# Reordering the loads at the start of a selective scan, and moving one copy from VectorE to ScalarE

## The chip, the cores and the metric

The kernel runs on one core of a Trainium2 chip. The metric is the device time of one execution in microseconds (us). The engines are TensorE (PE, matmuls), VectorE (DVE), ScalarE (ACT), GpSimd (POOL) and SyncE (SP); SP computes nothing here and issues most of the DMA transfers. Each engine works through its own instructions in order, and engines wait for one another by semaphores.

## The reference, cut to what matters

Two layers of a language model follow each other: a Mamba block with a 4-bit quantised feed-forward network, and an attention block with a mixture-of-experts network. The changed lines all lie in the Mamba block. It has two sequences (b = 0, 1) of 512 tokens with 512 features, 1024 inner channels and 16 states per channel:

```python
x = x + _layernorm(_L0_attn_ref(_layernorm(x), ...))      # the Mamba block, then three more
# inside _L0_attn_ref:
proj = hidden_states @ W_in.T
x, gate = (proj[..., :D_IN], proj[..., D_IN:])             # D_IN = 1024
xc = conv_b + sum(conv_w[:, j] * xpad[:, j:j + L, :] for j in range(4))
x = silu(xc)
ssm = x @ W_x.T
ts, Bm, Cm = rms(ssm[..., :32]), rms(ssm[..., 32:48]), rms(ssm[..., 48:])
dt = softplus(ts @ W_dt.T + b_dt)
def step(state, inp):                                      # over the 512 tokens
    dt_t, B_t, C_t, u_t = inp
    state = state * exp(dt_t[..., None] * A) + (dt_t * u_t)[..., None] * B_t[:, None, :]
    return state, einsum('bdn,bn->bd', state, C_t)
y = (ys + x * D) * silu(gate)
return y @ W_out.T
```

## The kernel before

Everything is in float32. Channels lie on the 128 partitions, so a sequence has 8 chunks of channels (c = 0 to 7), and tokens lie along the free dimension. The 16 states go in 8 groups (gi) of two. A scan step s handles one group of one chunk of one sequence: 2 x 8 x 8 = 128 steps.

*The head* runs before the scan and handles sequence 0: its tokens are loaded (`load_x(0)`, L83), normalised and transposed; for each chunk PE projects (L613), ACT and DVE do the convolution and the SiLU, and PE collects the "ranks" dt, B and C of all chunks in one PSUM bank. Beside it DVE, POOL and ACT dequantise words of the feed-forward weights and store them to DRAM (L233, L288, L299, L304). Gate 0 is projected in full (L639), and the first two of the four matmuls of gate 1 are done while DVE normalises the ranks (`half_gate`, L650). The normalised ranks are transposed on PE (L536). `ranks_out` (L539) then copies the dt rows to `dtT` on ACT (L541) and the B and C rows to `bc` on DVE (L542), and stores `bc` to DRAM as `scr` (L544). From there `states` (L547) loads each group of B or C back, broadcast to all partitions: 512 KB into a tile of 128 x 2 x 512. Sixteen of these transfers (eight B, eight C) are queued on SP one after the other; only group 0's product takes B from a matmul instead (`B0`, L688 to L693). Behind them on SP stand the four tiles of sequence 1's tokens (`load_x(1)`, L667) and then the loads of the last cut of the words. At most eight transfers of SP are in flight: each reuses one of eight semaphores and waits for the transfer eight places before it.

*The scan stage* goes through the 128 steps. For each step ACT takes two exponentials into PSUM (`exps`, L1033), DVE multiplies dt*u with B (`times_B`, L1049, reported at L1055) and runs the recurrence as one scan instruction over 1024 elements (`scan`, L1057, reported at L1059), POOL multiplies by C (`times_C`, L1063, L1065), and PE adds the groups up with identity matmuls (`sums`, L1075, L1087). Six `bx` buffers carry a step from DVE over POOL to PE; two `da` tiles carry the exponentials, so that those of step s + 2 wait for scan s. At each new chunk ACT copies dt to PSUM (`new_du`, L1043, L1047) and DVE multiplies it by u (L1053); `fin` (L1093) multiplies the finished chunk by its gate.

Beside the scan a generator (`stream`, L993) gives PE its other work for both sequences in pieces: the gates (`gate`, L751, matmuls at L741), each followed by three ACT instructions and a POOL product (`silu_of`, L712 to L719); the transposes of sequence 1 (L821); its projections; its ranks (`ranks1`, `rows1`, which call `ranks_norm` and `ranks_out` for b = 1); and, once the gates of sequence 0 are used, the output projection with weights `wo` (L897, L953) and the feed-forward network. The norm of sequence 1 (`norm_job`, L793) places one `bn_stats` (L798) on DVE every step from step 5 on. A rough budget (`STEP` = 3.5 us per step and `MM` = 0.86 us per matmul) decides how many pieces of the stream go into each step. In chunk 7 of sequence 0 the broadcasts of sequence 1's B and C follow, each as soon as its tile is free (L1152).

The order of the instructions on PE, ACT, DVE and POOL is exactly the order in which the program traces them (`pin`, L405). SP isn't pinned: `tc.issue_after` sets a lower limit for a transfer, and its place on the queue is found by the scheduler.

Of the kernel before, what the change touches and what calls it, by code (L numbers as in the profile page):

```python
# [18 lines left out]
P = 128  # L19
# [37 lines left out]
def tile_sandwich(  # L57
# [48 lines left out]
    wgt = const.tile([P, KH, NE], F32, name="wgt")  # L106


    def w4(src, name, chunks=KH, cols=PW):
        t_ = wst.tile([P, KH, PW], F32, tag="w4", name=name)  # L110
        nc.sync.dma_start(out=t_[:, :chunks, :cols], in_=src)
        return t_

    def moments(srcs, name):
# [311 lines left out]
    with ExitStack() as mamba:  # L426
# [21 lines left out]
        def mbank(name):  # L448
            return ps_m.tile([P, S], F32, tag="m", name=name)
# [18 lines left out]
        def w_in(part, b, c):  # L468

            key = "w", part, b, c // 2  # L470
            if key not in st:
                st[key] = w4(W_in[part * NCH // 2 + c // 2], f"w_{'xg'[part]}{b}_{c // 2}")
            return st[key]
# [28 lines left out]
        def ranks_norm(b, ps):  # L502

            sq = jrow(f"sq{b}")[:, : TB * N_ROW].rearrange("p (i r n) -> p i r n", i=TB, n=N_ST)
            nc.scalar.activation(sq.rearrange("p i r n -> p i (r n)"), ps, AF.Square)
            yield 2
            ss = stat.tile([P, TB, 3], F32, tag="ss", name=f"ss{b}")
            nc.vector.tensor_reduce(
                ss[:, :, 0], sq[:, :, : R_DT // N_ST].rearrange("p i r n -> p i (r n)"), AX.X, ALU.add
            )  # L510
            nc.vector.tensor_reduce(ss[:, :, 1:], sq[:, :, R_DT // N_ST :], AX.X, ALU.add)
            r = stat.tile([P, TB, 3], F32, tag="rr", name=f"rr{b}")
            nc.vector.tensor_scalar(r[:, :, 0], ss[:, :, 0], 1.0 / R_DT, 1e-6, ALU.mult, ALU.add)
            nc.vector.tensor_scalar(r[:, :, 1:], ss[:, :, 1:], 1.0 / N_ST, 1e-6, ALU.mult, ALU.add)
            yield 1
            if b:
                nc.gpsimd.tensor_tensor(r, r, mhalf3, ALU.pow)
            else:
                nc.scalar.activation(r, r, AF.Sqrt)
                nc.vector.reciprocal(r, r)  # L520
            yield 3
            nb = jrow(f"nb{b}")[:, : TB * N_ROW].rearrange("p (i r) -> p i r", i=TB)
            eng = nc.gpsimd if b else nc.vector
            eng.tensor_mul(
                nb[:, :, :R_DT], ps[:, :, :R_DT], r[:, :, 0:1].to_broadcast([P, TB, R_DT])
            )
            eng.tensor_mul(
                nb[:, :, R_DT:].rearrange("p i (r n) -> p i r n", n=N_ST),
                ps[:, :, R_DT:].rearrange("p i (r n) -> p i r n", n=N_ST),
                r[:, :, 1:3].unsqueeze(3).to_broadcast([P, TB, 2, N_ST]),  # L530
            )
            st["nb", b] = nb
# [6 lines left out]
        def ranks_out(b, pt):  # L539
            bc = st["bc"] = jrow(f"bc{b}")  # L540
            nc.scalar.copy(dtT[b][:R_DT, :], pt[:R_DT])  # L541
            nc.vector.tensor_copy(bc[R_B:N_ROW], pt[R_B:N_ROW])  # L542
            sc = dram.tile([N_ROW - R_B, S], F32, tag=f"scr{b}", name=f"scr{b}")
            nc.sync.dma_start(out=sc, in_=bc[R_B:N_ROW])  # L544
            scr.append(sc)
# [27 lines left out]
        with ExitStack() as p1:  # L573
            dq = pool(p1, "dq", 1)
            dz = pool(p1, "dz", 1)
            ps_1 = pool(p1, "p1mm", 2, PSUM)
            ps_r = pool(p1, "p1r", 1, PSUM)

            def bank1(i, name):
                return mbank(name) if i % 2 else ps_1.tile([P, S], F32, tag="mm", name=name)  # L580

            xT.append(xT_tile("xT0"))
            mvs, rn, xns, tps = {}, {}, {}, {}
            for i in range(TB + 2):
                if i < TB:
                    nm_ = f"m0_{i}"
                    mvs[i] = moments([x[i]], nm_)
                    rn[i] = rstd(mvs[i], nm_, 1)
                if 0 <= i - 1 < TB:
                    j = i - 1  # L590
                    rs = rn[j]
                    nm = minus_mean(mvs[j], rs, f"m0_{j}", 1)
                    xn = jrow(f"xn0_{j}")
                    apply(xn, x[j], rs, nm, 0)
                    tp = tps[j] = bank1(j, f"tp0_{j}").rearrange("p (k t) -> p k t", k=KH)
                    for kc in range(KH):
                        nc.tensor.transpose(tp[:, kc, :], xn[:, ts(kc, P)], ident)
                if 0 <= i - 2 < TB:
                    nc.scalar.copy(xT[0][:, :, ts(i - 2, P)], tps[i - 2])
            nc.scalar.activation(A, ch[:, :, KCONV + 2 :], AF.Exp)  # L600
            zds = zeros(dz, [gate_z, up_z], KH, INTER, "gu")

            apart = [f"gu{CUTS[1][0] * PW}_{j}" for j in range(PACK - 4, PACK)]
            gw.start(dq, zds, lambda n: new_g0(f"w_{n}") if n in apart else None)
            nc.vector.tensor_scalar(A, A, -1.0, None, ALU.mult)
            diag(0)

            pr = ps_r.tile([P, TB, S], F32, tag="psm", name="psm0")[:, :, :N_ROW]
            for c in range(NCH):
                w = w_in(0, 0, c)  # L610
                ps = bank1(c, f"px0_{c}")
                for k in range(KH):
                    nc.tensor.matmul(  # L613
                        ps, w[:, k, ts(c % 2, P)], xT[0][:, k, :], start=(k == 0), stop=(k == KH - 1)
                    )
                    if k == 1 and c >= 2:
                        for i in range(TB):
                            ranks_of(0, c - 2, i, pr)
                uc = u[0][c] = new_u(f"u0_{c}")
                evict_x(c, ps, uc)  # L620
                early = [gw.steps() for _ in range(4 if c == 0 else 0)]
                for word in early:
                    next(word)
                for word in early[:2]:
                    next(word)
                conv(c, ps, uc)
                nc.scalar.activation(uc, uc, AF.Silu)
                for word in early:
                    for _ in word:
                        pass  # L630
                if c:
                    gw.word()
                for _ in range((0, 0, 2, 0, 1, 0, 1, 0)[c]):
                    gw.word(nc.gpsimd)
            for i in range(TB):
                ranks_of(0, NCH - 2, i, pr)
            pg = mbank("pg0_0")
            for k in range(KH):
                nc.tensor.matmul(  # L639
                    pg, w_in(1, 0, 0)[:, k, 0:P], xT[0][:, k, :], start=(k == 0), stop=(k == KH - 1)  # L640
                )
            for i in range(TB):
                ranks_of(0, NCH - 1, i, pr)
            g[0][0] = new_g0("g0_0")
            nc.scalar.activation(g[0][0], pg, AF.Silu)

            root = stat.tile([P, 1], F32, tag="root", name="root", bufs=1)
            nc.scalar.activation(root, half[:, 0:1], AF.Sqrt)

            half_gate = mbank("pg0_1")  # L650
            for k in range(KH // 2):
                nc.tensor.matmul(
                    half_gate, w_in(1, 0, 0)[:, k, P : 2 * P], xT[0][:, k, :], start=(k == 0), stop=False
                )
            for _ in ranks_norm(0, pr):
                pass
            ranks_out(0, ranks_rows(0, bank1(0, "pt0")))

            for gi in range(NGI):
                if gi + 1 < NGI:  # L660
                    states(0, gi + 1, "B")
                states(0, gi, "C")
            last = states(0, 0, "B")
            gw.word()
            dt_out(0, 0, dt_in(0, 0, bank1(0, "pv0_0")))
            with tc.issue_after(last.ins):
                load_x(1)  # L667
            pin()

        g1p = pool(mamba, "mg1", 1)  # L670
# [4 lines left out]
        with ExitStack() as p2:  # L675
# [75 lines left out]
            def gate(b, c):  # L751
                w = w_in(1, b, c)
                if c + 2 - c % 2 < NCH:
                    w_in(1, b, c + 2 - c % 2)
                if (b, c) == (0, 1):
                    turns.append([f"pg{b}_{c}", None])
                    ps = half_gate
                    yield from in_proj(b, ps, w, c % 2, KH // 2)
                else:
                    ps = yield from bank(f"pg{b}_{c}")  # L760
                    yield from in_proj(b, ps, w, c % 2)
                spawn(gate_job(b, c, ps), 2)
# [717 lines left out]
```

## Time and profile before

| What | us |
|---|---|
| Median of 3 runs (957.22 to 958.73) | 957.5 |
| The profiled execution | 955.66 |
| Its span, first to last instruction | 953.7 |
| The head, up to the store of `bc` | 0 to 63.3 |
| Steps 0 to 7, with the first broadcasts | 68.0 to 104.5 |
| Transposes of sequence 1's ranks, DVE's copy of its B and C | 285.7 to 287.6 |
| Last step of sequence 0 on DVE | 326.4 to 328.6 |

The profile is of one execution. Its mean granted TensorE clock is 0.965 of full speed. Times within it are us from the start of the span. A row of a timeline reads: start, length, engine, line, operation, output <- input, count, and in brackets the idle time before it with what ended it. A name such as `bx` stands for all buffers of that name; `xN` counts instructions that were merged. A matmul of the program shows as two records. "SPq" is SP's issuing of a transfer, not the transfer. Tensor names carry no buffer numbers, so the n-th row of a group is told by its place in the order.

### The profile page before, as it was taken

To read this page: it belongs to the slowest core of one execution; us is meant where nothing else is said; L and a number is where in the kernel's file an instruction comes from. 1 tells how busy PE (TensorE), PEld (TensorE's weight loads), DVE (VectorE), ACT (ScalarE), POOL (GpSimd) and SP (SyncE) were. 2 spreads that over 40 slices of the span, in tenths; PEclk is the share of its full clock that TensorE was granted. 3 is DMA by queue.
4 is the path that set the end of the run, shared out by engine and by line. 5 is a ranking of instruction groups with operands and counts; after the bars stand their busy time and mean duration, and the time that the engine had idled before them with its cause. 6 is when DMAs were issued, how large, how long until landed. Compare 5 with 4: busy or idle time off the path is not lost.

```text
span 953.7 us, 7163 instructions
## 1 busy us (share of the span) xinstructions
PE 860.8 (90%) x2188; PEld 385.4 (40%) x2188; DVE 672.4 (71%) x780; ACT 424.1 (44%) x638; POOL 486.8 (51%) x356
## 2 busy tenths in 40 slices
PE   6989778789999889589999999999999998999994
PEld 3433333334533434134434444444544444455441
DVE  5877999999999998999999995535600024525225
ACT  4356675656666655476655640125320013412122
POOL 7746796677877787876877884440000000011002
PEclk9989999888999999889999999999999999999998
DMA  6449111010002854200111103445222231100101
GB/s 201 156 141 376 52 37 38 30 37 30 22 23 91 293 194 142 89 0 0 45 44 45 30 9 125 153 156 198 57 65 74 60 101 44 67 12 23 56 0 44
DMA packets 43816, 80.08 MB, mean 84 GB/s; under 512 B 7774, under 2 KB 20937, under 8 KB 43778
## 3 DMA queue, kind: packets, MB, share of 16 engines
q1 hardware_dynamic: 41506, 73.64, 23.4%
q0 software_dynamic: 1984, 5.47, 1.6%
q10 hardware_dynamic: 288, 0.52, 0.1%
q8 instruction: 17, 0.28, 0.1%
q14 instruction: 21, 0.17, 0.1%
HBM read 68.37 MB, written 11.24 MB: 83 GB/s over the span
## 4 chain that ended last, share of the span: by engine, by line
PE 48%; DVE 24%; issue 9%; POOL 7%; DMA 3%; ACT 2%; SPq 0%; DVEq 0%; POOLq 0%; ACTq 0%
DVE bx L1059 10%; DVE bx L1055 6%; PE py L1087 6%; PE pd L1408 6%; POOL bx L1065 5%; PE pup L1345 5%; PE fo L1198 4%; PE fg L371 4%; PE fu L371 4%; PE fo L1261 3%; PE fu L984 3%; PE fg L984 3%; PE po L1176 3%; PE po L953 2%; DVE u L483 2%
## 5 line engine op out<-in xcount | busy, mean ns | idle before, releaser
L1065 POOL TENSOR_TENSOR bx<-bx,C 128x1024 f32<-128x1024 f32 x128 | 301.8, 2358 | 117.4 <-DVE bx L1059 94.2
L1059 DVE TENSOR_TENSOR_SCAN bx<-da,bx 128x1024 f32<-128x1024 f32 x128 | 291.4, 2277 | 0.1
L1087 PE MATMUL py<-bx,ident 128*128 128x512 f32 x480 | 234.9, 620 | 41.4 <-POOL bx L1065 36.3
L1039 ACT ACTIVATE da<-dt,A 128x511 f32<-128x511 f32 x256 | 176.6, 691 | 170.1 <-DVE bx L1059 163.4
L1087 PEld LDWEIGHTS py<-bx,ident 128*128 128x128 f32 x480 | 90.8, 197 | 168.1 <-issue 91.7
L1055 DVE TENSOR_TENSOR bx<-du,B 128x1024 f32<-128x1024 f32 x127 | 152.8, 1203 | 5.7 <-DMA B<-scr 2.2
L1274 DVE TENSOR_TENSOR it<-it,fu 128x512 f32<-128x512 f32 (+1 forms) x11 | 7.5, 686 | 75.2 <-PE fu L371 75.2
L385 POOL TENSOR_TENSOR sd<-ve,half 128x4 f16<-128x4 f16 x2 | 2.1, 1042 | 110.7 <-DVE ve L383 110.7
L1345 PE MATMUL pup<-hT_l,wup 128*128 128x512 f32 x128 | 57.8, 606 | 0.0
L741 PE MATMUL pg<-xT,w_g 128*128 128x512 f32 x116 | 56.5, 619 | 0.0
L1408 PE MATMUL pd<-wdn,hid 128*128 128x512 f32 x128 | 55.3, 593 | 0.0
L127 POOL TENSOR_TENSOR rs_lo<-ve_lo,mhalf 128x1 f32<-128x1 f32 x8 | 5.4, 680 | 76.7 <-DVE ve_lo L125 76.7
L371 PE MATMUL fg<-hT_f,wg 128*128 128x512 f32 (+1 forms) x88 | 41.9, 614 | 0.7 <-ACT hT_f L171 0.7
L984 PE MATMUL fg<-hT_f,wg 128*128 128x512 f32 (+1 forms) x88 | 42.1, 597 | 0.0
L984 PE MATMUL fu<-hT_f,wu 128*128 128x512 f32 (+1 forms) x88 | 40.7, 592 | 0.0
L483 DVE SCALAR_TENSOR_TENSOR u<-px,ch,u 128x511 f32<-128x511 f32 (+2 forms) x48 | 35.8, 746 | 6.9 <-ACT u L476 5.8
L1261 PE MATMUL fo<-wd,it 128*128 128x512 f32 (+1 forms) x88 | 40.5, 603 | 0.0
L371 PE MATMUL fu<-hT_f,wu 128*128 128x512 f32 (+1 forms) x88 | 39.8, 593 | 0.0
L1198 PE MATMUL fo<-wd,it 128*128 128x512 f32 (+1 forms) x88 | 38.0, 594 | 1.8 <-DMA wd<-wd_d 1.8
L1408 PEld LDWEIGHTS pd<-wdn,hid 128*128 128x128 f32 x128 | 24.2, 190 | 30.7 <-issue 30.1
L1345 PEld LDWEIGHTS pup<-hT_l,wup 128*128 128x128 f32 x128 | 24.3, 193 | 28.8 <-issue 28.8
L1273 ACT ACTIVATE it<-fg 128x512 f32<-128x512 f32 (+1 forms) x11 | 6.6, 597 | 65.7 <-PE fg L371 65.7
(238 smaller groups left out, 1164.8 us busy)
## 6 DMA issues: line engine op xcount, KB each, us to landing
wo<-in_W_outT SPq DMA_DIRECT2D x20, 512.0 KB
B<-scr SPq DMA_DIRECT2D x16, 512.0 KB
C<-scr SPq DMA_DIRECT2D x16, 512.0 KB
wg<-wgu_d SPq DMA_DIRECT2D x10, 512.0 KB
wu<-wgu_d SPq DMA_DIRECT2D x10, 512.0 KB
w_x<-in_W_in SPq DMA_DIRECT2D x8, 512.0 KB
wgu_d<-w_gu POOLq DMA_DIRECT2D x16, 256.0 KB, 2.4
w_g<-in_W_in SPq DMA_DIRECT2D x8, 512.0 KB
```

The costliest lines, as they stand in the source:

```text
L371: nc.tensor.matmul(ps[:m], w[:, kc, e * P : e * P + m], hT[:, kc, :], start=(kc == 0), stop=(kc == KH - 1),)
L741: nc.tensor.matmul(ps, w[:, k, ts(e, P)], xT[b][:, k, :], start=(k == 0), stop=(k == KH - 1))
L984: nc.tensor.matmul(ps[:m], wt[j][a][:, kc, e * P : e * P + m], hT[:, kc, :], start=(kc == 0), stop=(kc == KH - 1),)
L1039: nc.scalar.activation(das[s % 2][:, i, 1:], st["dt", b, c][:, 1:], AF.Exp, scale=A[:, c, n : n + 1])
L1055: nc.vector.tensor_mul(bx, st["du"].unsqueeze(1).to_broadcast([P, NG, S]), Bbs[b][gi])
L1059: nc.vector.tensor_tensor_scan(flat, das[s % 2].rearrange("p n t -> p (n t)"), flat, 0.0, ALU.mult, ALU.add)
L1065: nc.gpsimd.tensor_mul(bxs[s], bxs[s], Cbs[b][s % NGI])
L1087: nc.tensor.matmul(st["y"], ident, bx[:, i, :], start=False, stop=last)
L1198: nc.tensor.matmul(fo[t], its[i][:m, ts(t, P)], w[:m, e], start=(i == 0), stop=(i == len(IC) - 1),)
L1261: nc.tensor.matmul(fo[t], its[i][:m, ts(t, P)], w[:m], start=(i == 0), stop=(i == len(IC) - 1),)
L1345: nc.tensor.matmul(ps, w[:, kc, ts(e, P)], src[kc], start=(kc == 0), stop=(kc == KH - 1))
L1408: nc.tensor.matmul(pd, hid[kc][:, ts(i, P)], wdn[kc], start=(kc == 0), stop=(kc == INT // P - 1),)
```

## The change

Four edits, all in the Mamba block:

- The tokens of sequence 1 are loaded behind the first gate weights (`issued[-1]` is then the load of `w_g0_0`), ahead of the stores and broadcasts of B and C. On SP's queue they move past two loads of gate weights, the store of `scr`, and sixteen broadcasts. The later loads of words and weights keep their order, but for one weight load (`w_x1_2`), which goes ahead of a store of dequantised words (L304) that was in front of it.
- The broadcasts of sequence 0 go B1, B2, C0, B3, C1, B4, C2, ..., B7, C5, C6, C7, B0 instead of B1, C0, B2, C1, B3, C2, ..., B7, C6, C7, B0.
- For sequence 1, `ranks_out` copies the B and C rows on ScalarE, right behind the copy of the dt rows, instead of on VectorE. On DVE the instruction stood between a product with B (group 5 of chunk 6) and the scan of group 4.
- Gate 1 of sequence 0 has three of its four matmuls in the head and one in the scan stage. On PE the last matmul of gate 2 then moves ahead of the dt matmul of chunk 1 (L562); all that follows has the order of before.

```diff
+    issued = []
+
     def w4(src, name, chunks=KH, cols=PW):
         t_ = wst.tile([P, KH, PW], F32, tag="w4", name=name)
-        nc.sync.dma_start(out=t_[:, :chunks, :cols], in_=src)
+        issued.append(nc.sync.dma_start(out=t_[:, :chunks, :cols], in_=src))
         return t_
...
             nc.scalar.copy(dtT[b][:R_DT, :], pt[:R_DT])
-            nc.vector.tensor_copy(bc[R_B:N_ROW], pt[R_B:N_ROW])
+            if b:
+                nc.scalar.copy(bc[R_B:N_ROW], pt[R_B:N_ROW])
+            else:
+                nc.vector.tensor_copy(bc[R_B:N_ROW], pt[R_B:N_ROW])
...
-            half_gate = mbank("pg0_1")
-            for k in range(KH // 2):
+            first_gate = mbank("pg0_1")
+            for k in range(KH - 1):
                 nc.tensor.matmul(
-                    half_gate, w_in(1, 0, 0)[:, k, P : 2 * P], xT[0][:, k, :], start=(k == 0), stop=False
+                    first_gate, w_in(1, 0, 0)[:, k, P : 2 * P], xT[0][:, k, :], start=(k == 0), stop=False
                 )
+            with tc.issue_after(issued[-1].ins):
+                load_x(1)
...
             for gi in range(NGI):
                 if gi + 1 < NGI:
                     states(0, gi + 1, "B")
-                states(0, gi, "C")
+                if gi:
+                    states(0, gi - 1, "C")
+            states(0, NGI - 1, "C")
             last = states(0, 0, "B")
             gw.word()
             dt_out(0, 0, dt_in(0, 0, bank1(0, "pv0_0")))
-            with tc.issue_after(last.ins):
-                load_x(1)
...
-                    ps = half_gate
-                    yield from in_proj(b, ps, w, c % 2, KH // 2)
+                    ps = first_gate
+                    yield from in_proj(b, ps, w, c % 2, KH - 1)
```

## The prediction

> **What bounds the kernel now.** I read the page first, then the waits of VectorE (DVE), then the timelines of SP, DVE, ScalarE (ACT), GpSimd (POOL) and TensorE (PE) around those waits. The page names PE, but as an average over stages:
>
> ```profile
> PE 860.8 (90%) x2188; PEld 385.4 (40%) x2188; DVE 672.4 (71%) x780; ACT 424.1 (44%) x638; POOL 486.8 (51%) x356
> PE 48%; DVE 24%; issue 9%; POOL 7%; DMA 3%; ACT 2%; SPq 0%; DVEq 0%; POOLq 0%; ACTq 0%
> ```
>
> The stretches (length, then busy us of PE, PEld, DVE, ACT, POOL, then granted clock) tell the stage that the change touches:
>
> ```profile
> 58.00:92.00 34.00, 32.06 (x70) 13.12 (x70) 23.59 (x27) 24.99 (x39) 19.33 (x12) 0.90 0.82 306
> 92.00:140.00 48.00, 36.68 (x91) 14.87 (x90) 47.53 (x40) 32.66 (x51) 37.76 (x23) 1.00 0.17 57
> 140.00:200.00 60.00, 51.13 (x111) 21.08 (x109) 58.79 (x50) 35.53 (x55) 42.36 (x27) 0.94 0.12 39
> 200.00:260.00 60.00, 52.88 (x144) 24.72 (x145) 59.52 (x44) 37.73 (x56) 45.60 (x25) 0.89 0.07 24
> ```
>
> From 92 to 260 DVE is busy 165.8 of 168 us: one scan step costs 3.31 us (a scan and a product with B, starts 78.06 and 81.37), and DVE alone sets the pace. So what DVE idles before 92 moves everything behind it. Its waits between 60 and 120, and between 260 and 300 (total, times, longest):
>
> ```profile
> DVE st_n L798 <- DMA x<-in_x_in: 3.5, 1, 3.5
> DVE bx L1055 <- DMA B<-scr: 2.2, 1, 2.2
> ...
> DVE bc L542 <- ACT dtT L541: 2.8, 1, 2.8
> ```
>
> These are the three places that the change works on: the statistics of sequence 1 wait for x, the product of group 2 waits for B, and the copy of sequence 1's B and C holds up a scan that doesn't need it.
>
> SP's timeline gives the rate of the broadcasts. After eight are in flight each issue waits for a landing, so its start marks one:
>
> ```profile
> 72.29 0.32 SPq L554 DMA_DIRECT2D C<-scr  x1
> 73.60 0.32 SPq L554 DMA_DIRECT2D B<-scr  x1
> 75.50 0.32 SPq L554 DMA_DIRECT2D C<-scr  x1
> 76.79 0.32 SPq L554 DMA_DIRECT2D B<-scr  x1
> 78.07 1.60 SPq L554 DMA_DIRECT2D C<-scr  x2
> 81.90 4.19 SPq L83 DMA_DIRECT2D x<-in_x_in  x4
> ```
>
> Read with the order B1 C0 B2 C1 B3 C2 B4 C3 B5: place 1 landed by 69.56, place 2 at 72.29, 3 at 73.60, 4 at 75.50, 5 at 76.79, 6 at 78.07, then one per 1.28 us: 8 at 80.63, 9 at 81.90, 10 about 83.2, 12 about 85.8, 16 about 90.9. x is behind all sixteen; its first tile ends a DVE wait at 91.53.
>
> **Part 1, loads.** The four x issues (about 0.35 us each, 1 MB) go on SP's queue behind the first gate weights (issued 30.83) and ahead of two weight loads, the store of B and C and sixteen broadcasts. They wait for old transfers only. The next weight load waits for PE and comes some 10 us later; DMA share in 32 to 38 is 0.25 to 0.63, so 1 MB (2.6 us at the broadcasts' rate) fits. The weights loaded beside it are used at 53; GpSimd's writes of dequantised words there could land a few us later, and have four buffers. I take 0, with 0 to 0.7 us of loss as bounds. The loads of the words' last cut and of the fourth gate weights, queued behind x before, move up by 2.6 us.
>
> **Part 2, order of B and C.** The order becomes B1 B2 C0 B3 C1 B4 C2 B5 C3 B6. B2 takes place 2, B3 place 4, B4 place 6, B5 place 8, B6 place 10. DVE by hand: the product of group 1 ends at 71.4; B2 lands 72.29, so the product of group 2 starts at 72.3 instead of 73.60, a gain of 1.30. At 3.31 us a step, B3 is wanted at 75.65 (landed 75.50), B4 at 78.95 (78.07), B5 at 82.3 (80.63), B6 at 85.6 (83.2). ScalarE's exponentials for group 3 end at 79.46, before its scan at 80.1. So the statistics, whose place is after the product of B6, start at 86.78 instead of 91.53:
>
> ```profile
> 73.60 1.22 DVE L1055 TENSOR_TENSOR bx<-du,B 128x1024 f32<-128x1024 f32 x1 [2.17 <-DMA B<-scr]
> 86.88 1.20 DVE L1055 TENSOR_TENSOR bx<-du,B 128x1024 f32<-128x1024 f32 x1
> 91.53 0.69 DVE L798 BATCH_NORM_STATS2 st_n<-x 128x6 f32<-128x512 f32 x1 [3.45 <-DMA x<-in_x_in]
> ```
>
> That is 3.45 + 1.30 = 4.75 us.
>
> [...] The trace shows landings one by one in the order of issue. [...] I take the row, 4.75.
>
> Who pays? C0 lands in place 3 (73.6, not 72.29), C1 76.8, C2 79.3, C3 81.9, C4 84.5. GpSimd by hand, products 2.33 and gates 1.25 each in their order: 73.7, gate, 77.3, gate, 80.9, gate, 84.5, then 86.85 (before: 72.44, 77.10, 80.64, 84.19, 87.04). It is 0.3 late and then early. PE wants the fourth product at 87.44; it is ready at 86.85. PE then has its own work until 94.3, so the sums of group 5 come at 94.3 instead of 97.09, those of 6 at 97.8, those of 7 at 102.4 instead of 107.20: 4.75 again. ScalarE waits at 90.28 for a gate's matmul, which delays the exponentials of group 7 to 93.2; their scan is at 97.5. The cover holds. If C0 came 2 us later still, GpSimd would push PE by under 2 us, given back by group 7.
>
> **Part 3, third matmul in the head.** PE idles 1.23 us before the transposes at 61.30; a matmul there is 0.86 us (four records, 58.14 to 60.08, are two), so it ends at 60.9. Of the block at 66.61 one matmul goes, but the next gate's fourth moves ahead of the dt matmul, so that stays sixth, at 73.41. Only the first gate's tanh gains, 0.8 us on ScalarE, for exponentials that aren't late. Clock rows here:
>
> ```profile
> 64.40:67.80 3.40, 3.40 (x5) 1.01 (x4) 1.80 (x4) 3.22 (x5) 2.24 (x2) 0.51 0.56 140
> 67.80:71.20 3.40, 3.40 (x6) 1.33 (x5) 3.36 (x4) 2.15 (x5) 0.00 (x0) 0.50 0.93 274
> ```
>
> Half clock. Were it full, PE would be some 2 us or more ahead, but DVE would still stand at B2. I take 0; bounds -0.4 (a late transpose) to +0.3.
>
> **Part 4, sequence 1's copy on ScalarE.** DVE now goes from the product at 282.86 straight into its scan, at 283.98 instead of 287.61: 3.6 us in hand (2.84 wait and the copy). ScalarE adds about 0.57 us (its neighbour, 32x512, takes 0.57) behind the wait for the transposes: exponentials of the scan after next at 287.4 to 288.8, wanted at 290.6. But the lead isn't kept. ScalarE's next tanh waits for PE, which works from 285.65 to 303 with 0.4 us of idle time and gains nothing from DVE's lead:
>
> ```profile
> 291.50 0.60 ACT L714 ACTIVATE th<-pg 128x512 f32<-128x512 f32 x1 [0.15 <-PE pg L741]
> ...
> 293.24 1.42 ACT L1039 ACTIVATE da<-dt,A 128x511 f32<-128x511 f32 x2
> 294.59 0.57 ACT L1047 COPY du<-dt 128x512 f32<-128x512 f32 x1
> ```
>
> Behind it stand exponentials (293.0) and the copy of dt for chunk 7 (294.35 to 294.95). DVE, done with its scan at 292.8, wants that copy: it waits 2.1 us, and starts du at 294.95 instead of 296.44. The gain is 1.5. Ends: 0.6 (the copy's own time) if PE lags more, 3.5 if PE catches up. I take 1.5, since the rows order it. The later steps follow: last product with C at 327.3 instead of 328.80, then the wo loads and PE's output projection, with 1.5.
>
> **Sum.** 4.75 + 0 + 1.5 = 6.25 us off the profiled execution (955.66 with a span of 953.7): 949.4. The median is 1.84 above that execution, so 957.5 - 6.25 = 951.2. Behind 331 PE is busy most of the time, in an order fixed by the program, each stage begun by the one before; nothing there starts by the clock on the wall, so the shift should arrive whole, with 1 us either way from DVE and GpSimd meeting at other moments.
>
> **Rivals.**
> *Transfers bind again (about 954).* B2 doesn't land earlier, or C binds GpSimd; only the 3.45 remains and the mid gain sinks under PE's lag: 957.5 - 3.45 = 954.0. For: B3's margin is 0.15 us, PE's for the fourth sums 0.6. Against: landings in strict order in SP's rows.
> *PE doesn't lag at 290 (949.2).* The whole 3.5 is kept: 957.5 - 8.25. Against: the 0.15 us wait of tanh says that PE is last there.
> [...]
> *It doesn't do what it says (957).* x goes early, but DVE then stops at the next late thing, GpSimd or PE at 94 to 102, for as long. Against: the hand schedule above.
>
> **Numbers.** As worked 0.70 (own range 949.3 to 953.2), full mid gain 0.09, transfers 0.12, no effect 0.05, clock 0.04. The range 948.2 to 954.8 holds the first three but for their ends. A measurement here tells 0.2%, 1.9 us, from no change: faster is under 955.6, which takes the first three nearly whole, 0.90; same 0.06; slower 0.04.
>
> **What would show it.** Right: no DVE wait for x; one B wait of about 0.9 us; statistics at about 86.8; GpSimd's first product with C near 73.7; no copy on DVE at 282, and a DVE wait of about 2 us for the du copy some 8 us later; du of chunk 7 about 6.2 us earlier than 296.44. Wrong: B2 still landing at 73.6; GpSimd busy without a gap and PE waiting for it past 100; du of chunk 7 earlier by under 4 us; or equal shifts at 330 and a smaller one at the end, with a lower clock.

## The result, and the profile after

The median went from 958.24 us (six runs) to 950.1 us (six runs, 947.58 to 953.17). The ratio of after to before is 0.9911, 95% interval 0.9888 to 0.9934: faster, by some 8 us. The profiled execution of after took 951.01 us with a span of 949.0, 0.9 us above the median of its kernel; that of before (955.66) was below the median of its own. So two single executions differ by 4.65 us where the medians differ by 8.1.

The totals and the chain's shares of after:

```profile
PE 862.2 (91%) x2188; PEld 386.3 (41%) x2188; DVE 672.1 (71%) x779; ACT 424.4 (45%) x639; POOL 486.8 (51%) x356
PE 50%; DVE 26%; issue 9%; POOL 6%; ACT 3%; DMA 0%; DVEq 0%; POOLq 0%; ACTq 0%
```

DVE has one instruction less and ACT one more, busy times are the same within 1.4 us, and of the chain's 3% of DMA nothing is left: the change took waits away, not work. (That 3% was the time in flight of a broadcast and of x on the chain, 12.3 and 9.6 us, and not the time to be gained.) The first two of the stretches that the prediction used (length, then busy us of PE, PEld, DVE, ACT, POOL, then granted clock):

```profile
58.00:92.00 34.00, 32.23 (x70) 13.11 (x70) 28.63 (x32) 25.10 (x40) 21.71 (x14) 0.90 0.78 295
92.00:140.00 48.00, 41.06 (x95) 16.61 (x94) 47.59 (x38) 35.69 (x55) 39.53 (x25) 0.93 0.13 44
```

Between 58 and 92 DVE is busy 28.63 us instead of 23.59; behind it DVE is full as before. The gain of the head is those 5.0 us. They are seen on SP, where the start of the tenth, eleventh and twelfth issue marks the landing of the second, third and fourth broadcast (now B2, C0, B3), and on DVE:

```profile
71.34 0.32 SPq L559 DMA_DIRECT2D B<-scr  x1
73.41 0.32 SPq L559 DMA_DIRECT2D C<-scr  x1
75.30 0.32 SPq L559 DMA_DIRECT2D B<-scr  x1
```

```profile
70.10 2.47 DVE L1062 TENSOR_TENSOR bx<-du,B 128x1024 f32<-128x1024 f32 x2
...
75.31 1.23 DVE L1062 TENSOR_TENSOR bx<-du,B 128x1024 f32<-128x1024 f32 x1 [0.54 <-DMA B<-scr]
...
86.38 0.69 DVE L805 BATCH_NORM_STATS2 st_n<-x 128x6 f32<-128x512 f32 x1
```

The products of groups 1 and 2 run back to back (x2): B2 had landed at 71.32, just in time. B3 was late by 0.54 us instead. The statistics no longer wait for x.

Around 285, first ScalarE, then DVE:

```profile
281.76 0.58 ACT L545 COPY bc<-pt 32x512 f32<-32x512 f32 x1
...
286.39 0.60 ACT L721 ACTIVATE th<-pg 128x512 f32<-128x512 f32 x1 [2.74 <-PE pg L748]
...
289.23 0.57 ACT L1054 COPY du<-dt 128x512 f32<-128x512 f32 x1
```

```profile
289.83 0.69 DVE L1060 TENSOR_TENSOR du<-u,du 128x512 f32<-128x512 f32 x1 [1.88 <-ACT du L1054]
```

The copy of sequence 1's B and C is on ScalarE. DVE's lead runs into the copy of dt for chunk 7, which stands on ScalarE behind a tanh that waited 2.74 us for PE, and DVE waits 1.88 us. DVE's instruction is still 6.61 us earlier than before, where it stood at:

```profile
296.44 0.67 DVE L1053 TENSOR_TENSOR du<-u,du 128x512 f32<-128x512 f32 x1
```

**How the kernels below are compared.** "Shift" is the start of the same DVE instruction in the profiled execution of before, minus its start in the other kernel's (positive is earlier), as a median over the stretch given. It comes from one execution each, so the medians of the runs stand beside it; the ratio is to runs of before on the same chip. "B2 landed" is counted from the landing of the store of `bc`. The trace records sixteen landings per transfer, and the last of them counts: in before those of B2 end at 73.16 (the fifteenth) and 73.58, and the product that waits for it starts at 73.60. The profiled execution of before was 2.6 us faster than the median of its kernel, which may be why the shifts read low beside the medians: order only has about the median of before, but a shift near -1.5.

| Kernel | B2 landed, us | First statistics | Shift 100-270 | Shift 314-329 | Shift at end | Median us | Ratio, 95% interval |
|---|---|---|---|---|---|---|---|
| before | 8.68 | 91.53 | 0 | 0 | 0 | 958.2 | 1 |
| after | 6.52 | 86.38 | 5.13 | 6.55 | 4.66 | 950.1 | 0.9911, 0.9888 to 0.9934 |
| after, again | 5.96 | 86.59 | 4.94 | 6.38 | 8.72 | 949.0 | 0.9911, 0.9875 to 0.9946 |
| early tokens only | 8.23 | 87.68 | 3.81 | 3.80 | 8.22 | 951.6 | 0.9931, 0.9904 to 0.9957 |
| order only | 8.04 | 92.92 | -1.44 | -1.48 | -1.60 | 957.7 | 1.0009, 0.9997 to 1.0022 |
| tokens and order | 8.43 | 88.54 | 2.96 | 2.92 | 2.56 | 952.3 | 0.9941, 0.9920 to 0.9962 |
| tokens and order, again | 5.53 | 86.89 | 4.63 | 4.60 | 3.78 | 951.9 (one) | |
| third matmul only | 9.42 | 91.90 | -0.39 | -0.39 | -2.19 | 957.9 (one) | |
| all but the copy | 5.49 | 86.40 | 5.12 | 5.11 | 3.14 | 951.0 | 0.9931, 0.9908 to 0.9955 |
| all but the copy, again | 5.97 | 86.03 | 5.47 | 5.46 | 4.37 | 951.3 (one) | |
| copy only | 8.37 | 91.56 | -0.07 | 1.34 | 0.33 | 955.2 | 0.9974, 0.9961 to 0.9988 |
| after, late store | 5.25 | 85.94 | 5.56 | 7.01 | 6.31 | 949.5 | 0.9922, 0.9891 to 0.9953 |
| after, later tanh | 5.83 | 85.76 | 5.75 | 8.56 | 8.36 | 949.4 | 0.9913, 0.9885 to 0.9941 |
| after, both | 5.42 | 86.51 | 5.01 | 7.84 | 7.36 | 947.8 | 0.9881, 0.9862 to 0.9900 |

A head that itself started late or early shifts a little as well: at 60 us the shift of these executions is already between -0.90 and +0.30, before any changed instruction could matter to DVE. "(one)" marks a single run, which has no interval.

### The profile page after: what moved, and what is told of

Its sections match the earlier page's. It is cut to its first block, busy times and chain, and to the rows that moved or that the text cites. A ratio compares the mean times of both kernels' runs of the same rounds, so it can differ in the third digit from the quotient of the medians.

```text
span 949.0 us, 7169 instructions
## 1 busy us (share of the span) xinstructions
PE 862.2 (91%) x2188; PEld 386.3 (41%) x2188; DVE 672.1 (71%) x779; ACT 424.4 (45%) x639; POOL 486.8 (51%) x356
## 3 DMA queue, kind: packets, MB, share of 16 engines
q0 software_dynamic: 1984, 5.47, 1.6%
## 4 chain that ended last, share of the span: by engine, by line
PE 50%; DVE 26%; issue 9%; POOL 6%; ACT 3%; DMA 0%; DVEq 0%; POOLq 0%; ACTq 0%
DVE bx L1066 10%; DVE bx L1062 7%; PE py L1094 7%; PE pd L1415 6%; PE pup L1352 5%; PE fo L1205 4%; POOL bx L1072 4%; PE fu L373 3%; PE fo L1268 3%; PE fg L373 3%; PE fu L991 3%; PE po L1183 3%; PE fg L991 3%; PE pg L748 2%; PE po L960 2%
## 5 line engine op out<-in xcount | busy, mean ns | idle before, releaser
L1281 DVE TENSOR_TENSOR it<-it,fu 128x512 f32<-128x512 f32 (+1 forms) x11 | 7.5, 686 | 72.3 <-PE fu L373 72.3
```

## The experiments

### Early tokens alone

```diff
+            with tc.issue_after(issued[-1].ins):
+                load_x(1)
...
-            with tc.issue_after(last.ins):
-                load_x(1)
```

> The kernel before with the early load of sequence 1's tokens alone; the broadcasts keep their old order. Theory (the parts of the head add up as worked out): the statistics of sequence 1 no longer wait for x, B2 still holds up DVE by about 2.2 us at 73.6, so the first statistics start near 88.1 instead of 91.53 and everything from 96 to 280 is 3.45 us earlier. Rival (x is not what gated, or its early load delays the broadcasts behind it): less than 2.5 us, with the DVE wait for B2 above 2.5 us. Rival (landing order is loose, order alone made the difference): the statistics already start at 86.8 or earlier here, as in the changed kernel.

The product of group 2 and the first statistics on DVE:

```profile
73.13 1.23 DVE L1057 TENSOR_TENSOR bx<-du,B 128x1024 f32<-128x1024 f32 x1 [0.54 <-DMA B<-scr]
...
87.68 0.69 DVE L800 BATCH_NORM_STATS2 st_n<-x 128x6 f32<-128x512 f32 x1
```

The statistics are 3.85 us earlier: the 3.45 us of the wait for x, and 0.47 because B2 came at 73.13 instead of 73.60, less 0.07. The bracket says 0.54 and not 2.2, because in this execution DVE came to it later (the four matmul records for `B0` took 3.77 us instead of 3.01, and its first product waited for them to 67.92, instead of 66.77), which costs nothing while B2 is last. The first theory holds. The early load delays no broadcast, nor the head, which at 60 us is within 0.03 us of before.

### The order alone

```diff
                 if gi + 1 < NGI:
                     states(0, gi + 1, "B")
-                states(0, gi, "C")
+                if gi:
+                    states(0, gi - 1, "C")
+            states(0, NGI - 1, "C")
```

> The kernel before with the new order of the broadcasts alone; x stays behind all sixteen. Theory: B2 lands by 72.3 and the product of group 2 starts 1.3 to 2.2 us earlier, but x still lands at 91.5, so the wait for x grows from 3.45 to 4.7 or 5.6 us and the shift from 96 on is 0. Rival (the two parts of the head are independent): the shift from 96 on is 1.3 us or more. Rival (C later makes GpSimd late and costs): from 96 on it is later than before by 0.5 us or more.

DVE's waits, 60 to 120 us (total, times, longest):

```profile
DVE st_n L800 <- DMA x<-in_x_in: 4.7, 1, 4.7
DVE bx L1057 <- DMA B<-scr: 2.2, 1, 2.2
```

No gain, as expected, and the time (1.0009) is that of before. But not for the reason given: B2, second in the queue, landed at 73.7, 8.04 us behind the store, hardly earlier than in third place. Fifteen of its sixteen landings were there by 71.26; the last came at 73.72. The shift of -1.44 holds 0.77 us of a late head; of the remaining 0.67, some 0.5 goes with the last landing, which stays 1.3 us behind the fifteenth in the transfers that follow (0.8 before), up to x. Whether the wait for x would swallow an early B2, this run couldn't show.

### Tokens and order, twice

Both diffs above together, with two matmuls in the head and DVE's copy.

> The kernel before with the early tokens and the new broadcast order, without the third matmul in the head and without the copy on ScalarE. Theory: statistics near 86.4, as in the changed kernel, a shift of 5.0 to 5.2 us from 96 to 280, and the same 5 us at 330, since DVE's copy of sequence 1's B and C still costs its wait at 284. Rival (the third matmul is what brings more than 4.75): a shift of 4.7 us or less. Rival (the copy is the larger part): the time is within 2 us of the kernel before.

```profile
74.15 1.23 DVE L1059 TENSOR_TENSOR bx<-du,B 128x1024 f32<-128x1024 f32 x1 [2.62 <-DMA B<-scr]
...
88.54 0.69 DVE L802 BATCH_NORM_STATS2 st_n<-x 128x6 f32<-128x512 f32 x1
```

A miss: 2.96 us instead of 5, hence less than the early tokens gained alone. Again fifteen landings of B2 were in by 71.52 and the sixteenth came at 74.13. Up to this run, the one new-order profile with an early B2, that of the changed kernel, had the third matmul, and the two with a late B2 did not. More runs were to tell that from chance; first the changed kernel unaltered, and all of it but the copy on ScalarE:

> The changed kernel once more, unaltered. Theory A (the second transfer's last sixteenth lands when it lands, and the place in the order settles only the other fifteen): B2 lands anywhere between 71.3 and 74.2 us, and the shift against the kernel before, from 96 to 280, is anywhere between 3.7 and 5.1 us. Theory B (the third matmul in the head, which the other runs did not have, brings B2 forward): B2 lands by 71.5 again and the shift is 5.0 to 5.2 us again.

> The changed kernel with sequence 1's B and C copied on DVE as before: three of the four edits. Theory: the shift at 330 is the shift at 280, without the 1.43 us that the changed kernel gains between 280 and 330; DVE waits about 2.8 us for the transposed ranks at 284. Theory A for the head: a shift of 3.7 to 5.1 us from 96 to 280; theory B: 5.0 to 5.2.

Both gave an early B2 (5.96 and 5.49 us) and 4.94 and 5.12 us of shift; so did the two later versions below. Five of five with the third matmul were early, as theory B wants it. (The part of the second kernel behind 280 is read below.) Then tokens and order without the third matmul were run once more, the third matmul alone, and all but the copy a second time:

> The early tokens and the new order without the third matmul, once more, unaltered. Theory A (a straggling sixteenth, by chance): B2 lands within 6.6 us of the store of B and C this time, as in the five profiles with the third matmul, and the first statistics start by 86.6. Theory B (the third matmul decides): B2 lands 8.0 us or more behind the store again, and the statistics start near 88.5.

> The kernel before with the third matmul of gate 1 in the head and nothing else. Theory: shift 0 within 0.3 us from 96 to 330 but for the offset of the head itself, since DVE stands at B2 and x whatever PE does; transposes of the ranks not late. Rival (theory B for the landing): the second transfer, here C0, lands within 6.6 us of the store and GpSimd's first product with C starts 1 us or more earlier than 72.44.

> Three of the four edits once more (early tokens, new order, third matmul; DVE still copies sequence 1's B and C), the neighbour of the repeat without the third matmul on the same chip. Theory A: B2 lands anywhere from 5.2 to 8.4 us behind the store, like without the third matmul. Theory B: within 6.6 us again, a sixth time.

Without the third matmul B2 now landed after 5.53 us, with DVE's two products in one row:

```profile
71.01 2.33 DVE L1059 TENSOR_TENSOR bx<-du,B 128x1024 f32<-128x1024 f32 x2
```

With the third matmul alone, the second transfer (C0 there) took 7.53 us. So theory B has fallen as it stood: the matmul is neither needed for an early landing nor enough. What is left is scatter of the last landing. In the ten profiles with the new order B2 took 5.25 to 6.52 us eight times and 8.04 and 8.43 twice; in the four with the old order, in third place, 8.23 to 9.42. The order brings B2 forward by some 2.5 us, in eight of these ten.

What holds up the last landing in the others isn't settled. It ran late over several us, not in one transfer alone: in tokens and order the last landing stays 1.4 to 1.8 us behind in the four broadcasts after B2, and the store of dequantised words from GpSimd's queue, moved beside them, has fifteen landings by 74.67 and the last at 76.84 (order only: 74.72 and 75.96; all but the copy: 74.32 and 74.38). Nor is it settled that this is chance alone. With the second transfer of the old order (C0, after 5.38, 6.22, 7.38 and 7.53 us) there are fourteen landings in second place. The four late ones, over 7 us, are three of the four kernels that load the tokens late and one of the ten that load them early; and in the new order all seven with the third matmul were early. Counts as small as these don't rule out that either edit changes the odds.

### The copy alone, and all but the copy

```diff
-            nc.vector.tensor_copy(bc[R_B:N_ROW], pt[R_B:N_ROW])
+            if b:
+                nc.scalar.copy(bc[R_B:N_ROW], pt[R_B:N_ROW])
+            else:
+                nc.vector.tensor_copy(bc[R_B:N_ROW], pt[R_B:N_ROW])
```

> The kernel before with sequence 1's B and C copied on ScalarE, nothing else. Theory (PE lags at 290 and the lead is given back to the wait for the du copy): shift 0 up to 280, 3.6 us at 283 to 290, a DVE wait of about 2 us for the du copy of chunk 7, and 1.5 us kept at 330. Rival (PE doesn't lag): 3.5 us kept at 330. Rival (only the copy's own time counts): 0.6 us. The end of the program differs from the shift at 330 by multiples of about 1.65 us where a half-clock stretch comes or goes.

```profile
295.04 0.70 DVE L1056 TENSOR_TENSOR du<-u,du 128x512 f32<-128x512 f32 x1 [2.08 <-ACT du L1050]
```

Before, this instruction stood at 296.44. The shift is -0.07 up to 280, 3.56 at 290 and 1.34 at 320. All but the copy gives the counterpart: 5.12 before and 5.11 behind, with DVE's wait for the transposed ranks back:

```profile
DVE bc L544 <- ACT dtT L543: 2.8, 1, 2.8
```

The two parts of the change add up: 5.12 and the copy's 1.34 + 0.07 make 6.53, against 6.55 for the whole.

### A later tanh

The wait that takes back DVE's lead can be moved: sequence 1's gate 4 is given to ScalarE two slots later, behind the copy of dt.

```diff
-            spawn(gate_job(b, c, ps), 2)
+            spawn(gate_job(b, c, ps), 4 if (b, c) == (1, 4) else 2)
```

> The changed kernel with the three ScalarE instructions of sequence 1's gate 4 two slots later, behind the exponentials and the copy of dt for chunk 7. Theory: the copy of dt no longer stands behind a tanh that waits for PE; the DVE wait of 1.9 us at 289.8 goes; PE's sums of chunk 6 still end at 299.2, so of the 1.9 us between 1.2 and 1.5 are kept at 330: there the changed kernel's gain of 1.43 us between 280 and 330 becomes 2.6 to 2.9. Rival (PE is the bound from 285 on): DVE's lead comes back as a wait for py at 299, and less than 0.4 us is kept. Rival (gate 6's matmul on PE waits for the bank that the late tanh still reads): PE stalls near 288.7 and the kernel is later at 330 than the changed one.

ScalarE and DVE:

```profile
284.03 1.41 ACT L1046 ACTIVATE da<-dt,A 128x511 f32<-128x511 f32 x2 [1.00 <-DVE bx L1066]
285.38 0.57 ACT L1054 COPY du<-dt 128x512 f32<-128x512 f32 x1
```

```profile
287.23 0.67 DVE L1060 TENSOR_TENSOR du<-u,du 128x512 f32<-128x512 f32 x1
...
298.59 0.69 DVE L1100 TENSOR_TENSOR g<-g,py 128x512 f32<-128x512 f32 x1 [0.51 <-PE py L1094]
```

DVE doesn't wait for the copy any more; it waits 0.51 us for PE's sums of chunk 6. Between 280 and 320 the gain is 8.56 - 5.75 = 2.81 us, against 1.42 in the changed kernel. That shows the cause of the wait: the order on ScalarE, with PE's lag as the next limit. The median, 949.4, doesn't tell 1.4 us from nothing.

### The last store of the head behind the broadcasts

```diff
-                (nc.sync if beside else nc.gpsimd).dma_start(
+            with tc.issue_after(late) if late and not beside else nullcontext():
+                (nc.sync if beside or late else nc.gpsimd).dma_start(
```

with `late` the last broadcast for the last word of the head, and nothing for the words ahead of it.

> The changed kernel with the store of the last dequantised word of the head moved from GpSimd's queue to SP's, behind the sixteen broadcasts. Theory (its 256 KB, moved at 71 to 74, take their share from the first broadcasts and hold back the last sixteenth of B2): B2 by 71.2, C0 by 72.8, B3 by 74.7, no DVE wait for B above 0.2 us, first statistics at 85.9 instead of 86.38. Rival (the broadcasts' own start is slow, the store is beside it): B2 scatters as in the other runs, and C0, B3 land within 0.3 us of 73.4 and 75.3, or later where B2 is later.

Counted from the store of `bc`, the fourth transfer, B3, lands after 9.03 us, against 9.57 to 10.48 in the new-order profiles without a late B2; that is near the 0.64 us that 256 KB take at the broadcasts' later rate (512 KB in 1.28 us). The last kernel below has the same edit, and B3 after 8.85 us. B2 landed earliest of all ten in these two, at 5.25 and 5.42, which hardly tells an effect from chance. C0 came at 73.59 and not at 72.8, in a head that was 1.0 us late. DVE has no wait for B, and the statistics stand at 85.94, as expected.

### Both

> The changed kernel with both later edits: the last word's store of the head behind the broadcasts, and sequence 1's gate 4 on ScalarE two slots later. Theory (their gains lie in different places and add): no DVE wait for B above 0.2 us, a shift of 5.6 to 5.8 us from 96 to 280 and of 8.4 to 8.6 at 330, against 6.4 to 6.6 in the changed kernel; the time about 2 us below the changed kernel, less than the scatter of its runs. Rival (PE gives the second gain back): 7.0 at 330, as with the late store alone.

The second gain is there (7.84 - 5.01 = 2.83 us), the first is not: with B out of the way DVE stops at the exponentials of group 3.

```profile
79.88 2.29 DVE L1069 TENSOR_TENSOR_SCAN bx<-da,bx 128x1024 f32<-128x1024 f32 x1 [0.76 <-ACT da L1049]
```

ScalarE was late because its softplus had waited 1.30 us for PE's dt matmul, which came behind a half-clock stretch (65.5 to 72.3): the ten matmul records of gates ahead of it took 7.40 us, the twelve behind it 5.42. So in these runs the next engine caps the head's gain near 5 to 5.8 us. At 0.9881 this is the fastest kernel measured, against 0.9911 twice for the change alone; the intervals overlap, so a gain over the change alone isn't shown.

## Why the prediction was right or wrong

**The total.** 951.2 us was predicted and 950.1 and 949.0 were measured. The 6.25 us of the sum are 6.55 and 6.38 in the traces at 320, where the changed part ends. The medians differ by more, 8.1 and 9.2 us. Part of that probably lies in the execution of before from which the shifts are counted (2.6 us faster than its median); how much of it comes from behind 331 is open. The prediction also subtracted from 957.5, the median of three runs; with more runs the median of before was 957.6 to 958.3. A base that was too low and a gain that was too small offset each other, so that the total came within 1.1 us is in part luck.

**Part 1, 3.45 us: right.** Alone it gave 3.81 of shift, of which 0.47 came from an earlier B2. Its cost of 0 held too.

**Part 2, +1.30 us: nearly the right sum from a wrong step.** The step was "B2 takes place 2, so it lands at 72.29", from the row "landings one by one in the order of issue". In the changed kernel B2 came at 71.32 and the gain there was 2.26 us, but B3, given a margin of 0.15, was 0.54 late: 3.45 + 2.26 - 0.54 = 5.17 against 5.15 measured (91.53 to 86.38). The risk was in the last landing: of the second transfer it came up to 2.6 us behind the fifteenth, and in two of ten profiles the place bought little or nothing. A head of 3.45 alone would have been too low for the usual case. Both belonged into the sum as a spread; the 72.29 was itself such a late last landing (at 72.28, with fifteen in by 70.53), read as the price of a place.

**Who pays: right.** GpSimd's first product with C started at 73.56 (worked out: 73.7), PE's sums of group 5 at 94.11 (94.3), of group 6 at 97.54 (97.8), of group 7 at 102.06 (102.4).

**Part 3, 0: right.** Alone its shift is -0.39, of which -0.18 was there at 60 us; the rest is within the 0.3 us that was allowed for, and B2 landed later too. That PE's half clock (0.50 from 64.4 to 71.2, in before and in the changed kernel) would not matter as long as DVE stands at B held: the waits for late exponentials were 0.3 us at most, and 0.76 only in the last kernel, where B was out of the way.

**Part 4, 1.5 us: right, with its mechanism.** 1.42 in the changed kernel, 1.41 alone, and the DVE wait of 2.1 us was 1.88. The later tanh showed that the wait ends on ScalarE's order.

**Behind 331, "the shift should arrive whole": wrong in a single execution.** Between 580 and the end it moves mostly by steps of about 1.65 us. In the changed kernel the first profile lost one (a shift of 6.30 ahead of it, 4.66 behind) at a stretch with a granted clock of 0.50 at 607, and the second, with a clock of 1.00 there, did not. In the traces of before and after the granted clock is either 1.00 or 0.50, and their eleven and thirteen stretches at 0.50 each start a whole multiple of 3.413 us after the first of the trace (64.48 and 64.41). Here are three kernels where PE waits for the weights `wd`, each in two neighbouring stretches of about that length (busy PE, PEld, DVE, ACT, POOL, then the granted clock). The changed kernel, whose wait is 2.62 us:

```profile
603.70:607.10 3.40, 0.78 (x3) 0.45 (x3) 2.73 (x6) 0.00 (x0) 2.05 (x3) 1.00 0.91 311
607.10:610.50 3.40, 3.40 (x6) 1.38 (x5) 2.26 (x7) 0.00 (x0) 1.49 (x3) 0.50 0.26 88
```

Third matmul only, with a wait of 2.03 us, and copy only, with 2.04:

```profile
610.73:614.14 3.41, 1.38 (x4) 0.49 (x3) 2.73 (x6) 0.23 (x1) 2.23 (x3) 1.00 0.95 331
614.14:617.55 3.41, 3.41 (x5) 1.35 (x4) 2.53 (x8) 0.00 (x0) 1.53 (x3) 0.50 0.21 72
```

```profile
608.17:611.58 3.41, 2.11 (x5) 0.57 (x3) 1.67 (x4) 1.34 (x3) 1.17 (x2) 1.00 0.48 160
611.58:614.99 3.41, 2.67 (x6) 1.25 (x7) 1.90 (x6) 0.00 (x0) 1.43 (x3) 1.00 0.63 233
```

Behind the first two waits the clock is 0.50, with six and five matmul records in the stretch; at 1.00 the repeat of the changed kernel has nine in 607.10 to 610.50. At the third, as long as the second, the clock stays 1.00: PE was busy for 1.38 us of the second's first stretch, and for 2.11 and 2.67 us of the third's two. So of two waits of the same length one was followed by half clock and the other was not; what decides it no run here shows. Nor does half clock follow idle time alone: in before PE is busy, with 32 short matmul records, for all of 866.61 to 870.02, and the clock is 0.50 from 870.02 to 873.43. From 580 on the changed kernel's first profile met four half-clock stretches that cost it time (607.13, 788.03, two from 863.13) and before's met three (695.94, 794.93, 870.02); the shift of the early tokens alone went from 4.76 at 450 to 8.22 at the end. The prediction gave the clock 0.04 as a cause of a slower kernel. The runs show such steps at 1.65 us each and with either sign: they scatter executions by several us and did not turn the sum.

The other rivals: transfers did not bind again at the size feared, except where the last landing straggled; PE does lag at 290, and the 8.25 us variant did not come; the change does what it says.

## What to carry to other kernels

A wait that disappears is worth its length only up to the next late thing, so list what is wanted next at the new pace (here B3, then the exponentials, then PE's sums) and compare each with its own arrival. A landing time read from one profile is one draw: look how far the last of its landings stands behind the others before building a step on it. When totals scatter by more than the effect, follow the same instruction through two traces: the shift shows where a gain begins, is given back, or is moved by something unrelated.

## What the runs showed of the hardware that was not expected

- The last of the sixteen landings of a 512 KB broadcast, the second in the queue, came between 0.03 us (early tokens alone) and 2.6 us (tokens and order) behind the fifteenth.
- The first broadcasts are slower than the later ones: landings in the changed kernel at 71.32, 73.39 and 75.28, then 1.3 us apart. All DMA together moves 168 to 381 KB per us from 67 to 72, and 406 to 426 from 74 to 76, in before, after, and tokens and order.
- A head that is up to 0.9 us late at 60 need not delay the scan: DVE's first product waits for PE, and that wait was 1.6 us in before and 0.6 to 0.8 us in the late heads of order only, tokens and order, the repeat of the changed kernel, and the late store.
- One stretch of 3.41 us at a granted clock of 0.50 (from 607.13 in the changed kernel, where PE is last) was a step of 1.65 us in all that followed. PE's wait for `wd` had one behind it when it took 2.03 us (third matmul only), and none when it took 2.04 us (copy only).
